# Layer 2 of a four-layer image network: two two-axis passes replaced by four one-axis passes on small array tiles, set between the next image's q, k and v

## The chip, the cores and the metric

The kernel runs on one core of one Trainium2 chip. The time is the device time of one execution in microseconds; the kernel before took 3720.93 us (median of three runs, 3720.22 to 3722.40). All data are float32, so every matmul on TensorE shows as two instruction records (two passes). The engines are called PE (TensorE), DVE (VectorE), ACT (ScalarE), POOL (GpSimd) and SP (SyncE, which issues most DMAs).

## The reference

Eight images of 512 channels and 32 x 32 pixels go through four layers:

```python
# layer 0
h = group_norm(x)                                  # 8 groups
q, k, v = split(qkv_w @ h + qkv_b)
h = softmax(q k^T / 8) v                           # 8 heads of 64
for _ in range(3):
    h = h + 0.1 * tanh(inl_w @ h + inl_b)          # the "inner loop"
x = x + proj_w @ h + proj_b
# layer 1
q, k, v = Wq @ x, Wk @ x, Wv @ x                   # q, k: 64 channels
x = x + v softmax(k-q scores)
# layer 2
out = x + bias
out = fir(fir(out, 2 * up_filter, up=2, axis=3), 2 * up_filter, up=2, axis=2)
out = leaky_relu(out, 0.2) * sqrt(2)
out = fir(fir(out, down_filter, down=2, axis=3), down_filter, down=2, axis=2)
# layer 3
rw = sigmoid(mean(out, pixels) @ router_w.T + router_b)     # 8 numbers per image
W = sum over e of rw[e] * experts[e]                         # mixed weights per image
... a bottleneck of three convolutions with W, three of batch normalization
```

Layer 2 treats each channel by itself: 32 x 32 pixels become 64 x 64, pass a leaky relu, and become 32 x 32 again. The filters have 12 taps. The same filter is used along both axes, so each pass can be done as one two-axis operator or as two one-axis operators.

## The kernel before

**Order of the work.** A loop over the images does layers 0, 1 and 2 of one image after another; layer 2's output z goes to DRAM ("spill"). Layer 3 follows for all images. Engines run concurrently, each through its own list of instructions. Where `tc.manual_schedule(engines=...)` stands, the listed engines keep the order in which the code is written; elsewhere a scheduler orders them.

**Products of 512 x 512 x 1024** (q, k, v, each inner step, proj, layer 1's values) use the seven products of Strassen's scheme in Winograd's form (`product`). They come in the order P1, C11, U2, U3, C22, C21, C12, each in two halves u = 0 and 1, and the generator yields after each of these 14 steps, so that callers can put other work between them. PE needs quarter sums of the operand (DVE) and copies of P1 (ACT). The accumulators are two banks of `ps_mm` (A) and the two double banks of `ps_sc` (X and Y); two more banks are in `ps_tp`. These eight banks are all of PSUM. Layer 1's weighted rows (`weighted_rows`) use the same scheme, written out.

**Layer 2 before.** The rows y (pixels x channels) are written to a padded copy in DRAM (`ypad`), and read back as overlapping blocks of 9 x 14 pixels with the pixels on the partitions (`Halo`). For each of 8 strips t of rows and 4 blocks c of columns one matmul with a 126 x 128 operator makes 8 x 16 fine pixels of 512 channels (`upsample`, L1139). ACT multiplies by 0.2 sqrt 2 and DVE takes the maximum (`leak`, L1122 and L1123). Then 256 matmuls per image, with the fine pixels as weights (128 x 64 tiles, two beside each other) and the down operator as moving data, add up into z with the channels on the partitions (`down_block`, L1157); an extra strip handles the last fine row. PE's order is written by hand: 3 strips up, rows down, 2 up, down, 3 up, down. The next image's statistics are made between layer 1's products, and q of the next image starts after layer 2.

**The experts.** Image b - 1's router and its mixed weights are made while q, k and v of image b run (`premix`): 9 pieces (the last of half the width), each of a 1 MB load on SP's queue, 16 scalings on ACT (L314) and additions on POOL (L319), with three pieces in flight. ACT and SP are in hand order there. The inner loop and proj of before have nothing beside them.

**Big buffers.** Tensors of 2 MB rotate through a pool of seven (`big_tile`); tensors of half a megabyte through six (`tmp`); weights through three.

Of the kernel before, what the change touches and what calls it, by code (L numbers as in the profile page):

```python
# [30 lines left out]
UR, UC = 8, 16  # L31
IR, IC = 9, 14
OR, OC = 9, 14
EDGE = 3
NT = 8
# [20 lines left out]
def tile_sequence(ctx: ExitStack, tc: tile.TileContext, a: dict, out: bass.AP, shifted: bool):  # L56
# [71 lines left out]
    up_op = const.tile([P, UR * UC], F32, name="up_op")  # L128
    up_left_op = const.tile([P, UR * UC], F32, name="up_left_op")
    dn_op = const.tile([P, OR * OC], F32, name="dn_op")  # L130
    up63_op = const.tile([P, P], F32, name="up63_op")
    nc.vector.memset(up63_op, 0.0)
    dn63_op = const.tile([P, 3 * W], F32, name="dn63_op")

    def layer2_constants():
# [5 lines left out]
        def scratch(name, n):  # L141
# [4 lines left out]
        counts = {  # L146
            "part": ([1, 1], 0, 1), "tap": ([1, NTAP], 0, 0),
            "first_in": ([IR, (P - 1) // IR], IR, 0), "first_up": ([UC, (P - 1) // UC], UC, 0),
            "first_in63": ([3, (P - 1) // 3], 3, 0),
            "ur": ([-1, UR], 17, 0), "uc": ([1, UC], 11, 0), "ucl": ([1, UC], 11 - 2 * EDGE, 0),  # L150
            "dr": ([2, OR], -6, 0), "dc": ([2, OC], 0, 0),
            "ur63": ([0, 1], 10, 0), "uc63": ([1, 2 * W], 5, 0),
            "dr63": ([2, 3], 1, 0), "dc63": ([2, W], 6, 0),
        }
        for name, (pattern, base, per_partition) in counts.items():
            t = counts[name] = scratch(name, pattern[1])
            nc.gpsimd.iota(
                t, [pattern], base=base, channel_multiplier=per_partition,
                allow_small_or_imprecise_dtypes=True,
            )  # L160

        taps_up, taps_dn = scratch("taps_up", NTAP), scratch("taps_dn", NTAP)
# [3 lines left out]

        def wide(t, n):
            return t.unsqueeze(1).to_broadcast([P, n, NTAP])

        def placed(name, idx, taps):  # L170
            n = idx.shape[1]
            t = scratch(f"placed_{name}", n)
            at = apart[:, 0 : n * NTAP].rearrange("p (n k) -> p n k", k=NTAP)
            nc.vector.tensor_tensor(
                at, idx.unsqueeze(2).to_broadcast([P, n, NTAP]), wide(tap, n), ALU.is_equal
            )
            nc.vector.tensor_tensor(at, at, wide(taps, n), ALU.mult)
            nc.vector.tensor_reduce(t, at, AX.X, ALU.add)
            return t

        tap, part = counts["tap"], counts["part"]

        def rows_of(name, width):

            row = scratch(f"row_{name}", 1)
            first = counts[f"first_{name}"]
            nc.vector.tensor_scalar(first, first, part, None, ALU.is_le)
            nc.vector.tensor_reduce(row, first, AX.X, ALU.add)
            col = scratch(f"col_{name}", 1)
            nc.vector.scalar_tensor_tensor(col, row, float(-width), part, ALU.mult, ALU.add)  # L190
            return row, col

        def tap_index(name, mul, by):

            t = counts[name]
            add = scratch(f"add_{name}", 1)
            nc.vector.tensor_scalar_mul(add, by, float(mul))
            nc.vector.tensor_scalar_add(t, t, add)
            return t

        def outer(op, rows, cols):
            nr, ncol = rows.shape[1], cols.shape[1]
            nc.vector.tensor_tensor(
                op.rearrange("p (r c) -> p r c", c=ncol),
                rows.unsqueeze(2).to_broadcast([P, nr, ncol]),
                cols.unsqueeze(1).to_broadcast([P, nr, ncol]),
                ALU.mult,
            )

        yield
        in_c, in_r = rows_of("in", IR)
        indices = {name: tap_index(name, -2, in_r) for name in ("ur",)}
        indices |= {name: tap_index(name, -2, in_c) for name in ("uc", "ucl")}  # L220
        yield
        up_rr, up_cc = rows_of("up", UC)
        indices |= {"dr": tap_index("dr", 1, up_rr), "dc": tap_index("dc", -1, up_cc)}
        yield
        in_c, in_r = rows_of("in63", 3)
        indices |= {
            "ur63": tap_index("ur63", -2, in_r), "uc63": tap_index("uc63", -2, in_c),
            "dr63": counts["dr63"], "dc63": tap_index("dc63", -1, part),
        }
        yield  # L230
        rows = {}
        for op, row, col, taps in (
            (up_op, "ur", "uc", taps_up), (up_left_op, "ur", "ucl", taps_up),
            (dn_op, "dr", "dc", taps_dn), (up63_op[:, 0 : 2 * W], "ur63", "uc63", taps_up),
            (dn63_op, "dr63", "dc63", taps_dn),
        ):
            if row not in rows:
                rows[row] = placed(row, indices[row], taps)
                yield
            cols = placed(col, indices[col], taps)  # L240
            outer(op, rows[row], cols)
            yield


    ypad = [
        spill.tile([(H + 5) * W, C], F32, name=f"ypad_{run}_{i}", tag=f"ypad_{i}") for i in range(2)
    ]


    rim0 = tmp("rim0")  # L250
    nc.gpsimd.memset(rim0, 0.0)
    def late_loads():
        nc.sync.dma_start(v_row, a["v_b"].partition_broadcast(P))
        nc.sync.dma_start(row_bias, a["bv"].partition_broadcast(P))
        nc.sync.dma_start(bias2, a["bias"].partition_broadcast(P))
        for t in ypad:
            nc.sync.dma_start(t[0 : 3 * W], rim0[0 : 3 * W])
            nc.sync.dma_start(t[(H + 3) * W :], rim0[0 : 2 * W])
# [17 lines left out]
    def route(b, parts):  # L276
# [4 lines left out]
        )  # L281
        nc.scalar.activation(rw[:, b, :], rw[:, b, :], AF.Sigmoid)

    def premix(b, halves=False):

        half, slots = NE // 2, 2 if halves else 3
# [4 lines left out]
        def load(i):  # L291
            at, n = pieces[i]
            slot = i % slots
            if slot < 2:
                views[i] = [read[:, slot, ts(h, half), 0:n] for h in range(2)]
                nc.sync.dma_start(read[:, slot, :, 0:n], a["experts"][:, :, at : at + n])
                return
            views[i] = [
                sums(f"experts_{b}_{i}_{h}").rearrange("p (e n) -> p e n", e=half)[:, :, 0:n]
                for h in range(2)  # L300
            ]
            for h in range(2):
                nc.sync.dma_start(views[i][h], a["experts"][:, ts(h, half), at : at + n])
# [68 lines left out]
    def channel_stats(b, x):  # L372

        stats = sums(f"stats_{b}")[:, 0 : CC * 2 * 6].rearrange(
            "p (c h s) -> p c h s", c=CC, h=2
        )
# [5 lines left out]
        return mv  # L382

    def norm_factors(b, mv):
# [8 lines left out]
        nc.vector.tensor_add(dev, dev, var_c)  # L393
        ps = bank(ps_tp, f"gn_var_{b}")
# [8 lines left out]
        return mul, add  # L403

    def group_norm(b, x, mul, add):
        h = big_tile(f"h_{b}", [P, CC, S])
        for cc in range(CC):
            nc.vector.tensor_scalar(
                h[:, cc, :], x[:, cc, :], mul[:, cc : cc + 1], add[:, cc : cc + 1],
                ALU.mult, ALU.add,  # L410
            )
        return h
# [267 lines left out]

    def layer0(b, x, norm, w):
        h = group_norm(b, x, *norm)
        if b == 0:
            first_sums(*held["q"], h[:, CC - 1, 0:1])
        t = quarter_sums(f"h_{b}", h)
        if b == 0:
            w["q"] = first_rest(*held["q"])
            for key in "kv":
                w[key] = weight_sums(key, *held[key], t[3][1][:, 0:1])
        fixed = tc.manual_schedule(engines={mybir.EngineType.Activation, mybir.EngineType.SP}) if b else nullcontext()  # L690
        with fixed:
            q = big_tile(f"q_{b}", [P, CC, S])
            parts = product(f"q_{b}", w["q"], h, t, channels(f"q_{b}", q, qkv_b[:, 0:CC]))
            for _ in range(2):
                next(parts)
            mixing = iter(())
            if b:
                mixing = premix(b - 1)
                next(mixing)
                route(b - 1, router_sums(b - 1))  # L700
            for _ in range(2):
                next(mixing, None)
            all_of(parts)
            if b == 0:
                nc.vector.tensor_add(row_bias, row_bias, bias2)
# [5 lines left out]
            for _ in range(2):  # L711
                next(parts)
# [178 lines left out]
    def layer1(b, x, w, midway):  # L891
# [112 lines left out]
        for t in range(3, NT):  # L1004
            halo.load(t)
# [517 lines left out]
```

## Time and profile before

| what | value |
|---|---|
| median of three runs | 3720.93 us (3720.22 to 3722.40) |
| the profiled execution: its own time | 3719.28 us |
| its span in the profile | 3717.5 us |
| granted TensorE clock, mean | 0.999 |
| busy: PE, DVE, ACT, POOL | 99%, 66%, 38%, 12% |
| from one image's q to the next image's | 436.25 us (890.93 to 1327.18) |
| DMA | 328.93 MB, 88 GB/s over the span |

The columns of a group of instructions are: line, engine, operation, output and inputs with their shapes, count, then busy time and the mean length of one in ns, then the idle time of that engine just before them with what ended it. In the chain of waits each row is a start, a length and what held the end of the program at that time. A row of the windows view is a stretch, its length, then for PE, weight loads, DVE, ACT and POOL the busy time and the count, then the granted TensorE clock, the DMA engines' busy share and the GB/s. Matmuls overlap their neighbours, so the mean length of one is more than the time that one adds.

### The profile page before, as it was taken

How to read it: one execution, taken by the hardware profiler on the slowest of the kernel's cores; microseconds unless marked ns; L12 is line 12 of the kernel's file. 1: busy time of each engine (PE TensorE's matmuls, PEld its weight loads, DVE VectorE, ACT ScalarE, POOL GpSimd, SP SyncE). 2: the span in 40 equal slices, each digit the busy share in tenths (PEclk: the TensorE clock that was granted, in tenths of full speed). 3: DMA queues.
4: the chain of work that ended last, by engine and by line, in shares of the span. 5: the costliest groups of instructions: out<-in, count | busy, mean ns of one | idle time of the engine just before them, and what ended most of it. 6: DMA issues, size and time to landing. Idle time of an engine off the chain costs nothing.

```text
span 3717.5 us, 51349 instructions
## 1 busy us (share of the span) xinstructions
PE 3687.2 (99%) x20742; PEld 1966.8 (53%) x20742; DVE 2440.0 (66%) x3412; ACT 1429.5 (38%) x2286; POOL 441.4 (12%) x586
## 2 busy tenths in 40 slices
PE   8999999999999999999999999999999999999998
PEld 4346753475435763467534764347543575347643
DVE  4887548665686657766487655866577664876454
ACT  1631255214552245322562136521454224631364
POOL 4000040001300040000400013000310004001031
PEclk9999999999999999999999999999999999999999
DMA  5002440125201350023501152013510235001763
GB/s 207 22 1 88 135 155 1 43 75 172 89 1 63 121 171 25 1 83 108 187 1 43 52 180 105 1 62 100 170 47 1 82 105 191 1 0 42 235 232 141
DMA packets 168583, 328.93 MB, mean 88 GB/s; under 512 B 12864, under 2 KB 112208, under 8 KB 162192
## 3 DMA queue, kind: packets, MB, share of 16 engines
q1 hardware_dynamic: 149952, 292.72, 23.3%
q0 software_dynamic: 4416, 19.99, 1.4%
q10 hardware_dynamic: 13968, 12.85, 1.0%
q8 instruction: 165, 2.70, 0.3%
q14 instruction: 82, 0.67, 0.1%
HBM read 256.70 MB, written 68.81 MB: 88 GB/s over the span
## 4 chain that ended last, share of the span: by engine, by line
PE 97%; DVE 2%; DMA 1%; ACT 0%; issue 0%; SPq 0%; ACTq 0%
PE scores L756 12%; PE av L797 12%; PE inl_X L527 6%; PE up L1139 5%; PE dn L1157 5%; PE v_X L527 5%; PE inl_Y L527 4%; PE av_X L1073 4%; PE inl_A L527 4%; PE v_Y L527 3%; PE av_A L1073 3%; PE v_A L527 3%; PE av_Y L1073 3%; PE proj_X L527 2%; PE q_X L527 2%; PE c L1339 2%
## 5 line engine op out<-in xcount | busy, mean ns | idle before, releaser
L775 ACT ACTIVATE e<-scores 128x1024 f32<-128x1024 f32 x504 | 516.1, 1024 | 441.7 <-PE scores L756 434.8
L756 PE MATMUL scores<-q,k 64*64 64x512 f32 x4096 | 531.9, 592 | 0.0
L797 PE MATMUL av<-e,v 64*64 64x512 f32 x4096 | 528.7, 589 | 0.0
L781 DVE TENSOR_TENSOR acc<-acc,e 128x1024 f32<-128x1024 f32 x320 | 389.2, 1216 | 36.7 <-ACT e L775 34.7
L319 POOL TENSOR_TENSOR experts<-experts 128x256 f32<-128x256 f32 (+2 forms) x297 | 237.8, 815 | 964.4 <-ACT experts L314 843.9
L756 PEld LDWEIGHTS scores<-q,k 64*64 64x64 f32 x4096 | 150.6, 133 | 295.3 <-issue 217.0
L797 PEld LDWEIGHTS av<-e,v 64*64 64x64 f32 x4096 | 156.6, 133 | 282.8 <-issue 277.2
L527 PE MATMUL inl_X<-T_hf,w_inl 128*128 128x512 f32 x576 | 261.8, 593 | 0.3 <-DVE inl_U L634 0.3
L314 ACT ACTIVATE experts<-experts,rw 128x256 f32<-128x256 f32 (+1 forms) x576 | 229.5, 483 | 80.1 <-DMA experts<-in_experts_dram 75.7
L1123 DVE SCALAR_TENSOR_TENSOR up<-up,leak 128x512 f32<-128x512 f32 x264 | 173.8, 687 | 128.7 <-ACT leak L1122 122.0
L959 POOL TENSOR_TENSOR seen<-seen,acc 128x512 f32<-128x512 f32 x16 | 20.2, 1264 | 1947.0 <-DVE acc L951 1946.4
L1122 ACT ACTIVATE leak<-up 128x512 f32<-128x512 f32 x264 | 149.8, 596 | 233.0 <-DVE up L1123 126.6
L818 DVE RECIPROCAL inv<-av 128x256 f32<-128x256 f32 x128 | 222.9, 1747 | 1.7 <-PE av L810 1.7
L1157 PEld LDWEIGHTS dn<-dn_op,up 128*64 128x64 f32 (+1 forms) x4096 | 187.9, 136 | 18.2 <-issue 18.2
L1157 PE MATMUL dn<-dn_op,up 128*64 128x99 f32 (+5 forms) x4096 | 194.1, 253 | 0.0
L623 ACT ACTIVATE inl_U<-inl_U,inl_b 128x512 f32<-128x512 f32 x96 | 66.7, 718 | 303.6 <-DVE inl_U L638 303.6
L527 PEld LDWEIGHTS inl_X<-T_hf,w_inl 128*128 128x128 f32 x576 | 108.6, 190 | 139.4 <-issue 114.5
L1139 PE MATMUL up<-halo,up_op 126*128 126x512 f32 (+1 forms) x384 | 179.7, 596 | 2.4 <-DVE up L1123 2.4
L527 PE MATMUL inl_A<-hf,w_inl 128*128 128x512 f32 x384 | 174.3, 596 | 0.0
L779 DVE TENSOR_TENSOR acc<-e,e 128x1024 f32<-128x1024 f32 x64 | 79.4, 1241 | 107.6 <-ACT e L775 77.3
L634 DVE TENSOR_TENSOR inl_U<-inl_X,inl_P 128x512 f32<-128x512 f32 x96 | 61.7, 684 | 105.1 <-PE inl_X L527 105.0
L527 PEld LDWEIGHTS inl_A<-hf,w_inl 128*128 128x128 f32 x384 | 71.6, 190 | 97.2 <-issue 86.1
(307 smaller groups left out, 5764.6 us busy)
## 6 DMA issues: line engine op xcount, KB each, us to landing
experts<-in_experts_dram SPq DMA_DIRECT2D x50, 1024.0 KB
halo<-ypad_u SPq DMA_DIRECT2D x128, 252.0 KB
halo<-ypad_u SPq DMA_DIRECT2D x128, 198.0 KB
w_v<-stored_u_v SPq DMA_DIRECT2D x14, 1792.0 KB
x<-in_x_dram SPq DMA_DIRECT2D x32, 512.0 KB
out_dram<-z SPq DMA_DIRECT2D x31, 512.0 KB
experts<-in_experts_dram SPq DMA_DIRECT2D x29, 512.0 KB
spill_u<-z SPq DMA_DIRECT2D x28, 512.0 KB
```

The costliest lines, as they stand in the source:

```text
L314: nc.scalar.activation(t[:, e, :], t[:, e, :], AF.Copy, scale=rw[:, b, which : which + 1])
L319: nc.gpsimd.tensor_add(dst, x, y)
L527: nc.tensor.matmul(dst, lhs, rhs, start=(opens and s == 0 and cc == 0), stop=(cc == 1 and s == rows), skip_group_check=True,)
L756: nc.tensor.matmul(ps[r][rows[c]], k[rows[r], oc, jc * P + c * HD : jc * P + c * HD + HD], q[rows[r], oc, ts(sh, HALF)], start=True, stop= ...
L775: nc.scalar.activation(e, pair, AF.Exp, scale=HD ** -0.5)
L781: nc.vector.tensor_add(accs[g], accs[g], e)
L797: nc.tensor.matmul(avs[g][r][rows[c]], v[rows[r], jc, ts(2 * oc + c, HD)], e[rows[r], ts(c, HALF)], start=(jc == 0), stop=(jc == SC - 1),)
L818: nc.vector.reciprocal(copies[g][:, at], totals[g][:, at])
L1073: nc.tensor.matmul(ps[:, ts(s, QR)], left[:, j, at : at + P], right[:, j, :], start=(what in ("P1", "U2", "W") and s == 0 and j == 0), sto ...
L1123: nc.vector.scalar_tensor_tensor(dst, ps, SQRT2, t, ALU.mult, ALU.max)
L1139: nc.tensor.matmul(ps[i], op[0 : IR * n, :], halo.tile(t)[0 : IR * n, c + i, :], start=True, stop=True,)
L1157: nc.tensor.matmul(rows[part, r0 - first : r1 + 1 - first, c0 : c1 + 1], up[t][0:k, c, ts(2 * cc + s, HD)], op[:, r0 - 4 * t + 3 : r1 + 4 ...
```

## The change

Layer 2 is done in four one-axis passes, by the class `Layer2`:

- `wide`: along the rows' pixels, 32 to 64. The operator is 32 x 64; eight matmuls of 32 x 64 array tiles (four row groups, two column groups) with 512 columns make one call, four calls make an image. The result goes to DRAM (`across`, two halves e of the channels) and comes back with the other axis on the partitions (`turn`).
- `up`: along the other axis, 32 to 64, eight units per image of eight 32 x 64 tiles each. ACT multiplies 128 x 1024 by 0.2, DVE takes the maximum (`tensor_max`), twice per unit.
- `down`: the same axis, 64 to 32, eight 64 x 32 tiles per unit, two units behind `up`. ACT copies one bank and DVE the other; the result goes to DRAM (`back`) and comes back turned (`turn_back`). `fine_passes` runs the units.
- `narrow`: along the first axis, 64 to 32, four calls of eight 64 x 32 tiles, copied by DVE; then `channels` transposes 128 x 128 blocks (32 per image) and ACT reads them out with the sum over pixels, which the router needs. `finish` runs both.

`between` sets these into the next image's work, with PE, DVE, ACT and SP in hand order: two wides inside `weighted_rows` (whose products come in a new order: P1, C11, U2, U3, C21, C22, C12), one before q, one after q's first step; `fine_passes` after q; k; `finish`; v, and the router after v's second step. For the last image `last_across` and `last_layer2` do the same with nothing in between.

The group norm of the next image is done in place on ACT instead of into a new tensor on DVE, and its statistics lie between the weighted rows' products. Because x is overwritten, it is loaded a second time for the residual of proj. The mixing of the experts of image b - 1 moves to the inner loop and proj of image b, one piece at every third product step, with two pieces in flight. The router's sigmoid is written ahead of it; in the built program ACT's list has it before the first exp of the attention, each with a load of its function table.

The core of the diff:

```diff
     def premix(b, halves=False):
-        half, slots = NE // 2, 2 if halves else 3
+        half, slots = NE // 2, 2
...
-        all_of(inner)
-        for it in (1, 2):
...
+        with tc.manual_schedule(engines=set(fixed)) if b else nullcontext():
+            mixing = iter(())
+            if b:
+                routed(b - 1)
+                mixing = premix(b - 1)
+                next(mixing)
+            slot = 0
+            def mix():
+                nonlocal slot
+                slot += 1
+                if slot % 3 == 2:
+                    next(mixing, None)
+            for _ in inner:
+                mix()
+            for it in (1, 2):
+                t = quarter_sums(f"hf_{b}_{it}", hf)
+                name = f"inl_{b}_{it}"
+                parts = product(name, w["inl"], hf, t, inner_step(name, hf))
+                for i, _ in enumerate(parts):
+                    mix()
...
+    def up(self, e, i):
+            n = 4 * e + i
+            pairs = []
+            for p in range(2):
+                if (2 * n + p) % 3 < 2:
+                    pair = ps_sc.tile([P, S], F32, tag="scores", ...)
+                    pairs.append(([pair[:, ts(r, HALF)] for r in range(2)], pair))
+                else:
+                    pairs.append(([bank(...) for r in range(2)], None))
+            for s in range(2):
+                for g in range(4):
+                    part = slice(W * g, W * g + W)
+                    first = 4 * i + 2 * s
+                    nc.tensor.matmul(
+                        pairs[g // 2][0][g % 2][HD * s : HD * s + HD, :], up_v[part, :],
+                        self.turned[e][part, first : first + 2, :], start=True, stop=True,
+                    )
+            fine = self.fine[n] = [tmp(f"fine_{self.b}_{n}_{p}", S) for p in range(2)]
+            for (banks, pair), t in zip(pairs, fine):
...
+                for dst, ps in parts:
+                    nc.scalar.mul(dst, ps, 0.2)
+                    nc.vector.tensor_max(dst, ps, dst)
...
+    def fine_passes(self):
+            order = [(e, i) for e in range(2) for i in range(4)]
+            lag = 2
+            for n in range(len(order) + lag):
+                if n < len(order):
+                    self.up(*order[n])
+                if n >= lag:
+                    e, i = order[n - lag]
+                    self.down(e, i)
+                    if i == 3:
+                        self.turn_back(e)
...
+    def between(b, eT, v, inv, y, x, w):
+        two = Layer2(b)
+        act, dve = nc.scalar.copy, nc.vector.tensor_copy
+        with tc.manual_schedule(engines=hand):
+            made, factors, stats = [], None, channel_stats(b + 1, x)
+            for what, u in weighted_rows(b, eT, v, inv, y):
+                if (what, u) in (("C11", 1), ("U2", 0), ("U2", 1), ("U3", 0)):
+                    mv = next(stats)
+                elif (what, u) == ("U3", 1):
+                    two.wide(0, 0, y, (ps_mm, ps_tp), (act, act))
+                    factors = norm_factors(b + 1, mv, made)
+                elif (what, u) == ("C21", 0):
+                    next(factors)
+                elif (what, u) == ("C22", 0):
+                    next(factors)
+                    two.wide(0, 1, y, (ps_mm, ps_tp), (act, act))
+                    two.turn(0)
+                elif (what, u) == ("C22", 1):
+                    group_norm(x, *made, nc.scalar)
+                    early_exp(b + 1)
+            two.wide(1, 1, y, (ps_mm, ps_tp), (act, dve))
+            t = sum_tiles(f"h_{b + 1}")
...
+            q, parts = queries(b + 1, x, t, w)
+            next(parts)
+            two.wide(1, 0, y, (ps_sc, ps_tp), (act, act))
+            two.turn(1)
+            all_of(parts)
+            w["inl"] = weight("inl", b + 1)
+            two.fine_passes()
+            k, parts = keys(b + 1, x, t, w)
+            all_of(parts)
+            w["proj"] = weight("proj", b + 1)
+            two.finish()
+            v, parts = values(b + 1, x, t, w)
+            next(parts)
+            sums_of = router_sums(b)
+            next(parts)
+            route(b, sums_of)
+            all_of(parts)
+            w["v1"] = weight("v1", b + 1)
+        return q, k, v
```

## The prediction

> **What bounds the kernel now.** I read the page first: its span, its busy line, the chain by engine and the costly groups.
>
> ```profile
> span 3717.5 us, 51349 instructions
> ...
> PE 3687.2 (99%) x20742; PEld 1966.8 (53%) x20742; DVE 2440.0 (66%) x3412; ACT 1429.5 (38%) x2286; POOL 441.4 (12%) x586
> ...
> PE 97%; DVE 2%; DMA 1%; ACT 0%; issue 0%; SPq 0%; ACTq 0%
> ...
> L775 ACT ACTIVATE e<-scores 128x1024 f32<-128x1024 f32 x504 | 516.1, 1024 | 441.7 <-PE scores L756 434.8
> ...
> L781 DVE TENSOR_TENSOR acc<-acc,e 128x1024 f32<-128x1024 f32 x320 | 389.2, 1216 | 36.7 <-ACT e L775 34.7
> ...
> L314 ACT ACTIVATE experts<-experts,rw 128x256 f32<-128x256 f32 (+1 forms) x576 | 229.5, 483 | 80.1 <-DMA experts<-in_experts_dram 75.7
> ...
> L1123 DVE SCALAR_TENSOR_TENSOR up<-up,leak 128x512 f32<-128x512 f32 x264 | 173.8, 687 | 128.7 <-ACT leak L1122 122.0
> ```
>
> TensorE is the bound everywhere: 99% busy, 97% of the chain. So only two things count: PE work that goes, and PE idle time that comes. Next, the chain of waits through layer 2 of image 3:
>
> ```profile
> 1271.92 3.47 PE av_X L1073 x16
> ...
> 1279.04 5.42 PE up L1139 x12
> 1284.46 8.46 PE dn L1157 x186
> 1292.92 7.07 PE up L1139 x16
> 1299.99 6.36 PE dn L1157 x128
> ...
> 1306.35 10.55 PE up L1139 x24
> ...
> 1327.18 7.20 PE q_A L527 x16
> ```
>
> The last av product ends at 1275.39 and q begins at 1327.18: 51.8 us, and 1.92 us of `up` ran earlier between the av products. So layer 2 holds PE for 53.7 us per image, nearly all of it work: 33 `up` matmuls of 0.86 us (28.4) and 24.2 of `dn`. The timeline of an attention stage shows what small tiles do:
>
> ```profile
> 1403.39 1.04 PE L756 MATMUL scores<-q,k 64*64 64x512 f32 x8
> ...
> 1404.25 1.04 PE L797 MATMUL av<-e,v 64*64 64x512 f32 x8
> ```
>
> Four 64x64 matmuls (two records each) start every 0.86 us, the time of one full-array matmul of 512 columns, and 1.04 us pass until the last ends. Last, two windows, q after layer 2 and an inner-loop step:
>
> ```profile
> 1327.00:1352.00 25.00, 25.00 (x65) 10.98 (x60) 11.21 (x19) 11.25 (x25) 10.16 (x13) 1.00 0.80 256
> 1545.00:1569.00 24.00, 24.00 (x57) 10.61 (x56) 16.12 (x27) 6.45 (x10) 0.00 (x0) 1.00 0.00 1
> ```
>
> PE (first pair after the span) is full in both; ACT (fourth) has slack, and DMA (the share before the GB/s) is 0.80 against 0.00.
>
> **The change part by part, per image.**
>
> *Removed:* the 53.7 us above. The halo reads and y rows, 9.5 MB, go too; they were hidden.
>
> *PE work added.* 4 wide calls, 8 up and 8 down groups, 4 narrow calls, each eight tiles of 32x64 or 64x32. A price for eight tiles is not in the trace. Low end: all eight together, 0.86, as four do; it can't be less, since 512 columns take two passes of 0.43 in every row. High end: four at a time, 1.73. I take 0.86: in the `dn` rows a record comes every 44 ns (8.46 us / 192), so issuing 16 in 0.86 us (54 ns) is no limit, and four tiles already run fully side by side. 24 groups are 20.6 us; 32 transposes at the xT row's 0.107 are 3.4. Sum 24.0, or 29.7 us less PE work than before.
>
> *Idle time added.* (a) The wides: 3.4 us of work; q's P1 can't have its banks before ACT and DVE have copied wide(1,1), two copies of 0.58 behind each other, so +1.3: 4.7.
>
> (b) Fine passes, between q and k with nothing else on PE. A unit needs two of the three PSUM pair buffers, so the second half of up(n+1) waits until DVE is through with pair 0 of up(n). The loop: semaphore to PE 0.055, the group to its last end 1.10 (1.04 above, plus four more starts), to ACT 0.07, `mul` of 128x1024 1.02 (L775's row), to DVE 0.03, `max` 1.25 (L781's 1.22; 1.26 to 1.29 where a 1024-wide operand came from PSUM): 3.5 us. Where pair 0 lies in two single banks (units 1, 4, 7) ACT and DVE overlap by halves, 3.15. DVE alone needs 2 x 1.25 and a copy of 0.65, 3.15; ACT 2.6. First max done 4.5 us after q, then 4 x 3.5 + 3 x 3.15 = 23.4, then the last max, down and its start 2.4: **30.3 us**, with 13.8 of PE work in it. So 16.5 of the 29.7 us saved come back here, as gaps of some 2 us.
>
> (c) Finish: 3.4 narrow, 3.4 transposes, 2.4 of waits for DVE's copies (0.65 each) and one ACT read: 9.2.
>
> (d) Experts mixing moves to the inner loop. Its cost in q, k, v was nil (PE full), so taking it out gains nothing. Its new slots: every third product step, 8 ACT scalings of 0.40 start to start, 3.3 us in front of whatever ACT does next. Most fall where ACT has 17 us free of 24. The one at slot 5 stands before the two copies of P1 that open inner step 1; DVE's quarter sums are due just then and PE's next product waits: 3.2 us. The one at slot 11, 0.65. Others, proj and their POOL adds (5.0 us a piece, POOL idle there) 0. If the expert load is late, ACT, which takes its queue in order, holds the tanh too; DMA is idle in that window and SP's eight extra issues have no one behind them until w_q, so 0. Bounds for (d): 0 (ACT catches up) to 8 (three chunks exposed).
>
> (e) The router's sigmoid now stands before the first exp of the attention: another table load on ACT, 1.28 us in its row, 1.0 on the path. Bounds 0 to 2.6.
>
> (f) Group norm goes from four DVE operations (0.80) to four on ACT (about 1.1), under av's products: 0. x is therefore read again, 2.1 MB and four SP issues, used 70 us later: 0. wide's writes, two turns and two returns are 16.8 MB instead of 9.5. q and its neighbours would move some 24 MB in 100 us, 240 GB/s, below the 256 that the window above shows. turn(1) lands about 22 us after q starts and q takes 26; turn_back(1) needs 12 us and k takes 24. Cost 0; with that cover gone, each microsecond late is paid once an image, up to 12 (0.5 MB written and 2.1 MB read at 256/0.80 = 320 GB/s are 8, and two landings 4, a guess).
>
> (g) The av products in a new order, C21 before C22 and C12, with the statistics of the next x (eight DVE operations of 0.67) between them: still 3.5 us of PE per product, and DVE has slack there, 0; were DVE late once, 1.3, one pair of its additions (0.69 each). Layer 2's operators of image 0 are fewer and lie under the inner loop as before, 0.
>
> Sum: 4.7 + 30.3 + 9.2 + 3.9 + 1.0 = 49.1 against 53.7, **-4.6 us** in each of seven images. The last image has no q and k to cover the turns: 3 for what is left of turn(0) after the wides, 12 for turn_back(1): 4.7 + 3 + 30.3 + 12 + 9.2 = 59, +5. Total -32 + 5 = -27 from the profiled execution's own 3719.28: 3692. The median, 3720.93, lies 1.65 above that execution, well inside the range.
>
> **A rule against the change.** The chain's very first q_A (14.76 us, after a nearly idle PE) took 10.19 us for sixteen records; the later one took 7.20. So this PE is slow after idling, and no later stage of before has a half idle PE. The Trainium skill, "TensorE: Matmul & The Clock Gate", Part 1, says that the clock halves after an idle window of about 3.4 us. By it gaps of 2 us cost nothing, and the sum stays. The same page's section on psum-queue depth-cycling says that frequent micro-idling between groups makes the clock oscillate. By that, (b) pays the first rival's price. No row of before decides between them.
>
> **Rivals.**
>
> *R1, slower: PE's clock drops in the fine passes.* For it: the slow first q_A. Against: gaps of 2 us, not 14. Price: the two passes of a group take 1.72 instead of 0.86, so the loop grows by 0.86 in 8 units, 7 us, and k starts cold, 3.0 (10.19 less 7.20): +10 an image, 80 in all, 3772. It decides from +3.4 an image (27 / 8), a third of that.
>
> *R2, slower: eight tiles go four at a time.* For it: nothing wider than four streams is shown, and all eight read their own 512 columns. Against: nothing in the spacing of `dn`. Price: 8 x 0.87 in the loop, 8 x 0.87 in wide and narrow, 14 an image: 3803. "TensorEngine Tiling (Array Packing)", Tiling Modes, of the Trainium skill, counts both shapes as eight independent tiles; by it R2 is out, and no row here shows it.
>
> *R3, about equal or a little slower: more chunks are exposed, or a turn is late.* For it: ACT, SP and DMA queues are all in order, and (d) and (f) are worked out with nothing late. 4 to 6 us an image more: 3720 to 3735, which includes the change not moving the time.
>
> *R4, much faster: the waits overlap better.* Fine passes at DVE's 3.15 a unit (28.5 in place of 30.3), the chunk of slot 5 hidden (3.2), half the waits of wide and finish (1.9): -7 an image more, 3645.
>
> **How the numbers follow.** Forecast as worked out 0.38 (3670 to 3710 by itself), R4 0.19, R3 0.16 (a quarter of it within 0.2%), R1 0.17, R2 0.10. A difference under 0.2% (7.4 us) can't be told from none here. Faster: 0.38 + 0.19 and a little of R1 with a clock that falls only now and then, 0.58. Same 0.04. Slower 0.38. Range: below 3625 only R4 with (e) hidden too; above 3785 R2 and a full R1 with late turns. So 3625 to 3785.
>
> **What the changed profile would show.** PE busy near 3687 - 8 x 29.7 = 3450, 93 to 94% of the span; `up` groups 3.1 to 3.5 us apart with idle ended by DVE's max; 8-tile groups of 16 records in 0.86 us; k's first products at the pace of q's; PE idle before inner step 1 ended by DVE or ACT; the granted clock at 1.00 in the fine passes (R1 wrong) or below; groups 1.7 us long (R2). I am wrong if idle shows up in q, k, v or the attention, where I have put none, or if `turned`/`back` reads end a wait.

## The result and the profile after

The changed kernel takes 4287.32 us (median of four runs, 4285.62 to 4290.46) against 3721.11 us. The ratio is 1.152, with a 95% interval of 1.150 to 1.154. The prediction was 3692 us in a range of 3625 to 3785, so it is wrong in sign, and even the dearest rival (3803) is nearly 500 us too cheap.

The span, the busy line and the chain by engine and line, from the page of the changed kernel:

```profile
span 4284.1 us, 48178 instructions
...
PE 3712.2 (87%) x19321; PEld 1789.4 (42%) x19321; DVE 2519.1 (59%) x3268; ACT 1535.6 (36%) x2399; POOL 528.3 (12%) x576
...
PE 64%; DMA 19%; DVE 9%; ACT 3%; SPq 3%; issue 1%; ACTq 0%; DVEq 0%
DMA across_u<-wide 12%; PE av L742 10%; PE scores L701 10%; DMA back_u<-sent 5%; PE inl_X L473 5%; PE v_X L473 4%; PE av_X L1014 4%; PE v_Y L473 3%; PE inl_A L473 3%; PE v_A L473 3%; PE inl_Y L473 2%; DVE T_hf L434 2%; PE c L1369 2%; SPq L1057 2%; PE dn L1103 2%; PE up L1080 2%
```

PE was 97% of the chain and is now 64%. The first name on the chain is no longer a matmul but a DMA, the write of the wide results to DRAM (`across`), and the write of the down results (`back`) is fourth: together some 700 us of waiting. Third comes DVE, with 9%.

Where in an image does it happen? In the timeline I took the first matmul of each stage, and from these starts the length of each stage. The table gives image 2 (images 1 to 7 are within 4 us of it in each stage). The columns e1, e8 and e9 are versions that are explained below; in e9 the first `up` stands inside q and the first narrows inside k, so that its rows from q to finish compare with the others only as a sum.

| stage, us | before | change | e1 | e8 | e9 |
|---|---|---|---|---|---|
| q | 24.5 | 44.6 | 27.2 | 25.4 | 21.9 |
| fine passes | - | 47.7 | 35.1 | 32.5 | 31.0 |
| k | 24.0 | 25.9 | 25.9 | 24.2 | 22.0 |
| finish | - | 21.4 | 9.1 | 9.1 | 11.8 |
| v | 24.3 | 26.2 | 26.1 | 24.5 | 24.5 |
| attention | 118.2 | 119.2 | 119.2 | 118.2 | 118.2 |
| inner steps, proj, layer 1's values and scores | 137.0 | 149.1 | 148.4 | 137.6 | 137.5 |
| transposes and first two weighted products | 19.2 | 19.3 | 19.3 | 19.3 | 19.3 |
| first av_X to the next q (before: with layer 2, 53.7) | 89.0 | 48.3 | 50.0 | 39.4 | 39.4 |
| sum | 436.3 | 501.7 | 460.3 | 430.1 | 425.7 |

The chain of the changed kernel between the weighted products and the second half of the fine passes, in order of time (start, length, what ended last):

```profile
1898.10 1.04 PE wide L1047 x16
...
1914.45 29.04 DMA across_u<-wide
...
1946.42 3.15 SPq L1057
1949.61 9.08 SPq L1057
1958.73 33.06 DMA across_u<-wide
1993.27 2.59 PE up L1080 x12
```

Two things stand here. The first row settles one rival at once: sixteen records of eight 32 x 64 tiles took 1.04 us, from the start of the first to the end of the last, as long as four 64 x 64 tiles. In the timeline the eight first passes start within 50 ns, and the eight second passes 0.43 us after the last of these. The other rows are waits of 29 and 33 us for writes of half a megabyte each, several behind one another. SP itself stands for 3 and 9 us on issuing such a write, with everything else in its queue behind it. The windows view says why (a stretch of 10 us during each write; the last two columns are the DMA engines' busy share and the GB/s):

```profile
1925.00:1935.00 10.00, 6.48 (x42) 2.28 (x43) 7.76 (x13) 2.42 (x5) 0.00 (x0) 0.99 0.13 53
1970.00:1980.00 10.00, 6.67 (x40) 1.92 (x38) 3.93 (x5) 1.02 (x1) 0.00 (x0) 0.96 0.13 54
```

The DMA engines are not busy: 0.13 is the share of two of sixteen. Nor do more writes at once help: four were issued between 1900.3 and 1920.2, and the rate stayed near 53 GB/s until the last had landed at 1943.6. The text before the prediction is wrong in one place: the generator `product` yields after each of its seven products, not after each of 14 halves; only `weighted_rows` yields 14 times.

### The profile page after: what moved, and what is told of

Read it like the earlier page. It is cut to its first block, busy times and chain, and to the rows that moved or that the text cites. A ratio compares the mean times of both kernels' runs of the same rounds, so it can differ in the third digit from the quotient of the medians.

```text
span 4284.1 us, 48178 instructions
## 1 busy us (share of the span) xinstructions
PE 3712.2 (87%) x19321; PEld 1789.4 (42%) x19321; DVE 2519.1 (59%) x3268; ACT 1535.6 (36%) x2399; POOL 528.3 (12%) x576
## 4 chain that ended last, share of the span: by engine, by line
PE 64%; DMA 19%; DVE 9%; ACT 3%; SPq 3%; issue 1%; ACTq 0%; DVEq 0%
DMA across_u<-wide 12%; PE av L742 10%; PE scores L701 10%; DMA back_u<-sent 5%; PE inl_X L473 5%; PE v_X L473 4%; PE av_X L1014 4%; PE v_Y L473 3%; PE inl_A L473 3%; PE v_A L473 3%; PE inl_Y L473 2%; DVE T_hf L434 2%; PE c L1369 2%; SPq L1057 2%; PE dn L1103 2%; PE up L1080 2%
## 5 line engine op out<-in xcount | busy, mean ns | idle before, releaser
L266 POOL TENSOR_TENSOR experts<-experts 128x256 f32<-128x256 f32 (+2 forms) x360 | 361.2, 1019 | 3044.7 <-ACT experts L261 3033.2
L720 ACT ACTIVATE e<-scores 128x1024 f32<-128x1024 f32 x504 | 516.1, 1024 | 384.6 <-PE scores L701 377.7
L1090 ACT ACTIVATE fine<-up 128x512 f32<-128x512 f32 (+1 forms) x168 | 127.6, 821 | 411.0 <-PE up L1080 259.4
L1091 DVE TENSOR_TENSOR fine<-up,fine 128x512 f32<-128x512 f32 (+1 forms) x168 | 156.2, 965 | 199.0 <-ACT fine L1090 194.9
L1080 PE MATMUL up<-turned,up_v 32*64 32x512 f32 x1024 | 141.4, 740 | 146.5 <-DVE fine L1091 124.4
L261 ACT ACTIVATE experts<-experts,rw 128x256 f32<-128x256 f32 (+1 forms) x576 | 230.6, 484 | 53.0 <-DMA experts<-in_experts_dram 47.7
L473 PE MATMUL inl_A<-hf,w_inl 128*128 128x512 f32 x384 | 185.6, 625 | 1.2 <-ACT inl_P L575 1.2
L1055 ACT COPY wide<-wide 128x512 f32<-128x512 f32 x110 | 58.0, 595 | 354.1 <-PE wide L1047 292.0
L473 PE MATMUL q_X<-T_h,w_q 128*128 128x512 f32 x192 | 100.8, 674 | 96.1 <-DVE q_U L505 96.1
L1136 PE MATMUL narrow<-back,dn_h 64*32 64x512 f32 x512 | 43.8, 771 | 113.5 <-DMA back<-back_u 113.5
L1155 ACT ACTIVATE z<-zT 128x1024 f32<-128x1024 f32 x32 | 32.6, 1022 | 298.2 <-PE zT L1151 256.1
L1080 PEld LDWEIGHTS up<-turned,up_v 32*64 32x64 f32 x1024 | 31.4, 149 | 252.8 <-DVE fine L1091 177.8
```

The source lines that it names most:

```text
L261: nc.scalar.activation(t[:, e, :], t[:, e, :], AF.Copy, scale=rw[:, b, which : which + 1])
L266: nc.gpsimd.tensor_add(dst, x, y)
L473: nc.tensor.matmul(dst, lhs, rhs, start=(opens and s == 0 and cc == 0), stop=(cc == 1 and s == rows), skip_group_check=True,)
L720: nc.scalar.activation(e, pair, AF.Exp, scale=HD ** -0.5)
L1080: nc.tensor.matmul(pairs[g // 2][0][g % 2][HD * s : HD * s + HD, :], up_v[part, :], self.turned[e][part, first : first + 2, :], start=True ...
L1090: nc.scalar.mul(dst, ps, 0.2)
```

## Experiments

Each version was timed once, and e8 (a second time) and e9 in five runs, which agree within 0.12%.

**e1: the writes split by their outermost count.** A wide result is written with 2 x 64 rows of 4 KB, a down result with 4 x 32. The experiment writes the same bytes in pieces that have 64 and 32 rows outermost:

```diff
-                nc.sync.dma_start(dst[:, :, first : first + S], t)
+                for h in range(2):
+                    nc.sync.dma_start(dst[h][:, first : first + S], t[ts(h, HD), :])
...
-            nc.sync.dma_start(dst[:, :, ts(i, S)], self.sent[e][:, ts(i, 4), :])
+            for g in range(4):
+                nc.sync.dma_start(dst[g][:, ts(i, S)], self.sent[e][ts(g, W), ts(i, 4), :])
```

> The changed kernel, with each write of a wide result issued as 2 DMAs of 64 rows and each write to back as 4 DMAs of 32 rows, the same bytes to the same places. Theory A (a DMA whose outermost count is 2 or 4 is spread over 2 or 4 of the 16 DMA engines; the trace shows a busy share of 0.13 and 53 GB/s during the wide writes): the shares rise, the waits on these writes go, 18 us in q, 17 in the fine passes, 12 in the finish and 4 of a slow clock in k and v per image, some 130 us in the last image: about 3800 us. Theory B (the writes are slow because of DRAM or of their 4 KB rows): no change, 4280. Theory C (PE, ACT and DVE themselves are slow in the fine passes): the waits on DMA go but the fine passes stay above 40 us: above 4000.

Measured: 3912.17 us, 375 less. The stages q, fine passes and finish fall by 17.4, 12.7 and 12.4 us per image, and the stretch from the last image's q to the end, which holds two layer 2s, by 117. The DMA issues of e1's page (KB each, then us from issue to landing):

```profile
across_u<-wide SPq DMA_DIRECT2D x128, 256.0 KB, 3.6
...
back_u<-sent SPq DMA_DIRECT2D x256, 128.0 KB, 2.3
```

Three times as many DMAs, the same bytes, and the median one lands in 3.6 and 2.3 us. Theory B, that DRAM or the 4 KB rows make the writes slow, is out, and so is theory C: the fine passes fall to 35.1 us. The kernel is still 5% slower than before, so this is not the only cause. Theory A had 3800: it was 112 us too low, because k and v did not recover, the fine passes stayed 4 us above my figure, and the last image's own layer 2, for which I had put 130, gave 74.

**e2: only the wide results' writes split.**

> As the one before, but only the writes of the wide results are split; the writes to back still have an outermost count of 4. Theory A: the finish still waits about 12 us per image for back, and the last image 40: 3900 to 3960 us. Theory B: 4280.

Measured: 4029.84 us, 70 us above the range, of the same sign; the finish still takes 21.7 us. This kernel shows the writes to `back` by themselves. The DMA view of 1430 to 1475 us, in 40 slices (busy share in tenths, then GB/s):

```profile
DMA  2110189999622222222222222222102999999999
GB/s 106 76 51 11 35 233 381 333 367 311 216 108 102 102 109 106 106 102 109 106 106 102 109 106 106 102 117 106 69 4 56 228 356 360 370 350 437 408 484 428
```

In the middle the writes with four rows outermost run alone: a share of 0.2 to 0.3, 102 to 109 GB/s. With two outermost it was 0.13 and 53. The reads on both sides, with 128 partitions outermost, run at 0.9 and 330 to 480. So for counts of 2 and 4 the rate goes with the outermost count, some 26 GB/s for each.

The Trainium skill states a rule for this, on which the prediction did not draw. "DMA: Bandwidth & Descriptors", in the section on why a DMA increments its semaphore by 16, says that a DMA is spread over the largest number of engines up to 16 that divides the slowest dimension of both sides, and its rules for kernel authors ask for a multiple of 16 outermost. The traces agree for 2 (0.13) and 4 (about 0.25).

**e3: e1 without most of POOL's additions.** Five of six additions per piece of the mixing are left out for images 0 to 6, so the mixed weights are incomplete:

```diff
             def added(dst, x, y):
-                nc.gpsimd.tensor_add(dst, x, y)
+                if halves or dst is mixed_to:
+                    nc.gpsimd.tensor_add(dst, x, y)
...
+            mixed_to = None
...
+            mixed_to = dst
             added(dst, lo[:, 0, :], lo[:, 1, :])
```

> The first kernel of this call, and in the mixing of images 0 to 6 five of six POOL additions per piece are left out (the mixed weights are incomplete); loads, ACT scalings and the writes stay. Theory A for the inner loop (POOL's additions slow DVE's quarter sums, which go from 0.68 to 1.21 us each beside them): the three inner steps fall from 83 to about 70 us per image, 85 us less than the first kernel in all. Theory B (ACT's scalings stand in front of the copies that open a step): no more than 20 us less in all, inner steps above 80.

Measured: 3855.64 us, 57 less than e1; the inner steps take 77.1 us in most images, proj 21.1. Both theories hold in part. From the inner steps to layer 1's scores the sum is 141.0 to 142.7 us (mean of seven images 141.5), against a mean of 150.3 in e1 and 137.0 before: the scalings, with the one addition that is left, cost 4.5, near the 3.9 that I had predicted, the other additions another 9. The timeline of the changed kernel shows their mechanism:

```profile
1734.13 3.28 ACT L261 ACTIVATE experts<-experts,rw 128x256 f32<-128x256 f32 x8
1735.17 1.28 DVE L434 TENSOR_TENSOR T_hf<-hf 128x512 f32<-128x512 f32 x2
1735.89 6.21 POOL L266 TENSOR_TENSOR experts<-experts 128x512 f32<-128x512 f32 x5 [13.16 <-ACT experts L261]
...
1738.05 1.21 DVE L434 TENSOR_TENSOR T_hf<-hf 128x512 f32<-128x512 f32 x1
...
1738.18 2.08 PE L473 MATMUL inl_X<-T_hf,w_inl 128*128 128x512 f32 x2 [3.48 <-DVE T_hf L434]
1739.18 1.21 DVE L434 TENSOR_TENSOR T_hf<-T_hf,hf 128x512 f32<-128x512 f32 x1
```

The two quarter sums that began before POOL did take 1.28 us together; of those beside it one takes 1.75 and the others 1.21 each, and POOL's five additions take 6.2 instead of 4.2 to 4.8. PE then waits 3.48 us for DVE. DVE's reads from PSUM are not slowed (`inl_U` takes 0.68 us in the changed kernel, beside POOL's additions as without them). That is what the Trainium skill, "SBUF — State Buffer", section "Who interferes with whom", states of a DVE operation with two inputs in SBUF beside GpSimd's reads.

**e4: e1 with a product on the other double bank after U2.**

```diff
-            ("U3", "X", s3, t3), ("C21", "X", a22, t4), ("C22", "Y", s1, t1),
+            ("W", "Y", s1, t1), ("C22", "X", s3, t3), ("C21", "X", a22, t4),
             ("C12", "Y", s4, b22),
```

The wide calls and the statistics inside the products move along with the new order.

> The first kernel of this call, with layer 1's weighted products in the order P1, C11, U2, W, C22, C21, C12, so that a product on the other double bank lies between U2 and the next product on U2's bank. Theory A (in the new order that next product waits until DVE, late behind sums and statistics, has read U2): the stretch from the first av_X to q falls by 8 to 10 us per image, 55 to 75 us less than the first kernel. Theory B (DVE is simply overloaded there by the statistics): less than 3 us per image.

Measured: 3892.18 us, 20 less; the stretch from av_X to q is only 1.6 us shorter. That is theory B's figure, but not its reason, which the timeline of this kernel contradicts:

```profile
1287.47 0.69 DVE L988 TENSOR_TENSOR av_U<-av_X,av_P 128x512 f32<-128x512 f32 x1
...
1288.21 5.41 PE L1014 MATMUL av_X<-T,S 128*128 128x256 f32 x16 [3.28 <-DVE av_U L988]
...
1306.31 0.69 DVE L993 TENSOR_TENSOR av_W<-av_X,av_W 128x512 f32<-128x512 f32 x1 [4.00 <-PE av_X L1014]
...
1307.05 3.72 PE L1014 MATMUL av_X<-v,eT 128*128 128x256 f32 x16 [0.67 <-DVE av_W L993]
```

PE waits before five of the ten half products on the double banks (3.28 us once, 0.67 to 0.78 otherwise), also where DVE had been idle for 4 us. The five are those that follow another half product on the same double bank directly; with a product on the other bank or a wide call in between there is no wait. The two halves of a double bank are one tile of the program, and the product on the one half waits until DVE has read the other. My theory had looked at whole products; the wait is between halves.

**e5: half of C22 between U2 and U3, in q, k and v.**

```diff
+            matmuls(which, (1,) if apart and what == "C22" else (0, 1))
+            if apart and what == "U2":
+                matmuls(4, (0,))
```

> The kernel with all writes split (e1), and in q, k and v of images 1 to 7 the first half of the product C22 (on the other double bank) is issued on PE between U2 and U3. Theory A (the hand order of PE put U3 right behind U2 on the same double bank, where before the scheduler had set half of C22 between; PE waits there for DVE's two additions): q, k and v each 1.4 to 1.9 us shorter, k at 24.1 and v at 24.3 us as in the kernel before, 30 to 40 us in all against e1. Theory B (k and v are slow from a PE clock that the fine passes and the finish leave low): no change in k and v, 25.9 and 26.1.

Measured: 3874.12 us, 38 less; q, k and v are 1.7 us shorter each, k 24.2 and v 24.5. Theory A holds, and a slow clock is out. In the kernel before, PE was not in hand order in these stages, and its trace has `k_Y` x4 between two groups of `k_X` x8: the scheduler had filled this wait.

**e6: the weighted products alternate by halves.**

```diff
+        for pair in (("P1",), ("C11",), ("U2", "W"), ("C22", "C12"), ("C21",)):
+            for u, what in [(u, what) for u in range(2) for what in pair]:
```

The order of the two channel halves e in layer 2 is exchanged, the statistics stand at other products, and the wide calls stand after W, C12 and C21.

> The kernel with all writes split (e1), and layer 1's weighted products alternate between the two double banks by halves (U2, W, U2, W, C22, C12, C22, C12, C21, C21), with the channel halves exchanged and the wide calls moved along. Theory A (a product may not write one half of a double bank before DVE has read the other; each pair in a row on one double bank costs 0.7 us, and 3.3 where DVE is late): the stretch from the first av_X to q falls from 48 to 51 to about 39 to 41 us, 60 to 75 us in all against e1. Theory B (DVE's work itself is the limit in that stretch): less than 3 us per image.

Measured: 3840.88 us, 71 less, and the stretch takes 40.9 us: theory A. DVE's operations are the same, so it is not their amount. Nor is it the wide calls that moved: in e1's trace (image 2) PE waits 7.1 us for DVE in this stretch and 0.74 for the copy of a wide, in e6's 0.67 for the copy of a wide and not for DVE. Where the clock does not fall behind the longest wait, e1's stretch takes 48.3 us, which is 7.4 more.

**e7: the nine pieces of the experts at other steps.**

```diff
-                if slot % 3 == 2:
+                if slot in (1, 2, 8, 9, 15, 16, 22, 23, 24):
```

> The kernel with all writes split (e1), with the same nine pieces of the experts mixed at other product steps: two in the middle of each inner step and three in proj, after the steps U2 and U3 (C22), where ACT has no copy or tanh due and DVE's quarter sums are not running. Theory A (the cost comes from where the pieces fall: scalings ahead of the copies of P1, POOL's additions beside the quarter sums): the three inner steps fall from 82.5 to 68 to 71 us per image, 80 to 100 us in all against e1. Theory B (ACT or POOL or the loads cannot keep this pace anywhere in the inner loop): above 77.

Measured: 3829.50 us, 83 less. The inner steps take 73.7 us against 66.5 before, and proj with layer 1's values less than before (boundaries move, since more work overlaps), in sum 137.5 against 137.0. The whole mixing costs 0.5 us where it no longer stands before the copies of P1 and all but one of its additions in an image miss the quarter sums, which are back at 0.684 us each. The one addition begins while DVE's quarter sums are under way, and there it is POOL that waits: 3.33 us instead of 1.28, and the four quarter sums beside it keep their 0.68. (In e3 one addition beside six quarter sums takes 4.08 us instead of 0.73 in the same way.) Here the quarter sums of the changed kernel:

```profile
L434 DVE TENSOR_TENSOR T_hf<-hf 128x512 f32<-128x512 f32 x128 | 106.4, 846 | 0.0
...
L434 DVE TENSOR_TENSOR T_hf<-T_hf,hf 128x512 f32<-128x512 f32 x64 | 62.7, 980 | 0.0
```

and of e7:

```profile
L434 DVE TENSOR_TENSOR T_hf<-hf 128x512 f32<-128x512 f32 x128 | 85.6, 684 | 0.0
...
L434 DVE TENSOR_TENSOR T_hf<-T_hf,hf 128x512 f32<-128x512 f32 x64 | 43.8, 684 | 0.0
```

**e8: all of these together**, with the sigmoid in v and a double bank of its own for the last but one down unit.

```diff
             route(b, sums_of)
+            routed(b)
+            early_exp(b + 1)
...
+            if n == 6:
+                pair = ps_sc.tile([P, S], F32, tag="scores", name=f"dn_{self.b}_{n}")
```

> All of these together (split writes, half of C22 between, alternating products, moved pieces), the router's sigmoid and the exp table's load in v instead of ahead of the attention (1 us), and the last but one down unit in a double bank of its own (1.5 us). If the effects add up: per image 461 less 10, 5, 13, 1 and 1.5, about 431; in all 3912 less 210: 3690 to 3720, about the kernel before.

Measured: 3690.15 us against 3718.56 for the kernel before, and a second time:

> The kernel with all changes (e8) again, timed against the kernel before in five rounds: 0.987 to 0.994 of the time before, as in its single execution (3690 against 3719 us).

3689.01 us, a ratio of 0.992 (0.990 to 0.993). The effects add up to what was expected (430.1 us per image for 431). Fine passes still took 32.5 us, and the windows of this kernel show part of the reason (the third column from the right is the granted clock):

```profile
1291.00:1297.20 6.20, 3.40 (x33) 0.77 (x32) 3.76 (x4) 1.94 (x2) 0.00 (x0) 1.00 0.78 291
1297.20:1301.30 4.10, 4.08 (x27) 0.94 (x32) 2.51 (x3) 2.00 (x3) 0.00 (x0) 0.52 0.03 11
1301.30:1305.00 3.70, 3.70 (x33) 0.83 (x34) 2.64 (x4) 2.53 (x4) 0.00 (x0) 0.61 0.00 0
1305.00:1312.00 7.00, 7.00 (x66) 1.50 (x66) 6.07 (x8) 5.27 (x8) 0.00 (x0) 1.00 0.59 149
```

PE works for 3.4 of the first 6.2 us, then runs at half its clock for about 7 us, and recovers while the passes go on. This happens in each of the seven images, and the longest gap between PE's records in these passes is 2.3 us (2.6 in one image).

**e9: the start and the end of the passes covered by q's and k's own products.**

```diff
+            for _ in range(5):
+                next(parts)
+            two.up(1, 0)
             all_of(parts)
...
+            two.fine_passes(begun=True, within=opened)
+            k, parts = k
+            for _ in range(5):
+                next(parts)
+            two.narrow(1, 0)
+            two.narrow(1, 1)
             all_of(parts)
```

`opened` issues k's first product ahead of the last down unit.

> The kernel with all changes (e8), and: the first up unit stands before q's last product C12 (on PSUM buffers that are free there), k's first product stands before the last down unit, and the first two narrow calls stand before k's last product. In e8 the fine passes take 32.5 us and the first units run at a granted clock of 0.52 to 0.61, after PE was idle for 2.8 of 6.2 us. Theory A (the passes start and end with PE waiting on ACT and DVE, and the idle start is what lowers the clock): the idle time is covered by q's and k's own products, the clock stays at 1.00, and an image takes 5 to 8 us less: 3635 to 3655 us. Theory B (any passes with PE half busy lower the clock; the dip only moves): 2 to 4 us per image, 3660 to 3676.

Measured: 3653.08 us (3650.25 to 3654.36), a ratio of 0.982 (0.980 to 0.983) to the kernel before, 36 less than e8, 4.4 per image in the table, a little below theory A's figure per image, and inside its range for the whole. Its fine passes in image 3:

```profile
1285.00:1293.00 8.00, 6.71 (x67) 1.25 (x66) 6.46 (x8) 5.46 (x9) 0.00 (x0) 1.00 0.52 211
1293.00:1301.00 8.00, 8.00 (x80) 1.76 (x80) 7.10 (x9) 5.73 (x9) 0.00 (x0) 1.00 0.66 171
1301.00:1309.00 8.00, 8.00 (x75) 2.25 (x70) 7.62 (x11) 5.60 (x9) 0.00 (x0) 1.00 0.58 156
```

The clock stays at 1.00 here and in images 1 and 6. In images 2, 4, 5 and 7 it falls to 0.5 for 3.4 us, some 10 us after the first `up`. Two windows of image 2:

```profile
857.00:861.80 4.80, 3.14 (x34) 0.65 (x32) 3.42 (x6) 2.00 (x3) 0.00 (x0) 1.00 0.69 239
861.80:865.20 3.40, 3.40 (x35) 0.55 (x25) 1.91 (x3) 2.34 (x3) 0.00 (x0) 0.50 0.48 205
```

With such a fall the passes take 30.7 to 31.2 us, without it 30.3. In the 3.4 us before these four falls PE's records cover 1.8 to 2.0 us, and 0.8 to 1.3 before the seven of e8. So the idle start did lower the clock, and covering it took away most of the slow time, but not all: theory B is not out, since passes with short gaps (at most 1.2 us in e9) still lower the clock in some images. The 4.4 us are waits that are now covered and a better clock together; no run separates them.

**e10: e9 with the writes joined again**, the diff of e1 taken back.

> The fastest version (e9) with the writes to DRAM joined again as in the change: outermost counts of 2 and 4. Theory A (the writes alone make the change slower than the kernel before, whatever the orders on PE and DVE): the 375 us that splitting gained in the changed kernel are lost again, all or nearly all of them: 3960 to 4060 us. Theory B (much of that was hidden waiting behind the other stalls, or is covered now because the turns are issued earlier): below 3850.

Measured: 4126.82 us, 474 more than e9, above the whole expected range. The writes alone make this design slower than the kernel before, and cost more where less else is waited for: here the finish waits 18 us instead of 12.

## Why the prediction was wrong, point by point

- **(f), the transfers: "Cost 0".** This is the step that failed. Of the 70 us by which a middle image missed (501.7 for 431.7), some 42 went when these writes were split (e1). I divided bytes by time (240 GB/s) and compared with what the trace had shown for other DMAs (256). That rate belongs to DMAs with 128 partitions outermost. These writes have 2 or 4 there and ran at 53 and 104 GB/s. The upper bound of 12 us went by the same kind of rate, so it was no bound. In the last image, where nothing covers the writes, the stretch from the first av_X to layer 3 grew by 90 us over before, for the 5 that I had put; in e1 by 16.
- **(g), the new order of the weighted products: 0, at most 1.3.** Wrong: 7.1 us of waits, and some 9 on average with the slow clock that follows the longest of them in four of seven images of e1 (e6). The step looked at DVE's slack, but not at what follows what on one double bank once PE is in hand order. The same reason cost 1.7 us in each of q, k and v (e5), which the prediction didn't list at all.
- **(d), the mixing: 3.9.** The scalings' part was nearly right (4.5 in e3); POOL's additions, put at 0, cost 9 by slowing DVE's quarter sums. The bound of 8 was too low. The rows of before hardly show it, since there most of POOL's additions lay beside reads from PSUM; but three 128 x 1024 sums of image 0's attention, whose two inputs are in SBUF, ran beside POOL and took 2.11 to 2.19 us instead of 1.22.
- **(b), the fine passes: 30.3.** 35.1 in e1. The loop is in the traces as worked out: once the passes run, a unit follows every 3.3 to 3.4 us in e1, for 3.15 to 3.5. Missing were the slow clock of the first units and the last three down units, which wait for one another's copies (e8's double bank for one of them gained at most 2.6 us).
- **(a), (c) and (e).** Finish 9.1 for 9.2, sigmoid 0.98 for 1.0. With the orders of (g) and e5 put right, the wides cost what was worked out: in e8 the stretch before q and q together take 5.0 us more than before without its layer 2, for 4.7. Taking the last image alone, e8 waits 14 and 6 us for its two turns, for 12 and 3.
- **R1, the clock.** In part right. Most of the slow clock of the change (its mean is 0.943, e1's 0.982) comes from the long waits for DMAs. But in e8 the clock fell in the fine passes without a gap above 2.6 us, so of the two places of "TensorE: Matmul & The Clock Gate" that were weighed, the one on an idle window of 3.4 us would not have foretold it, and the one on frequent micro-idling fits better. The price of R1 was too high: k starts at its usual pace in e8 (24.2 us), and in e9 a fall costs 0.4 to 0.9 us.
- **R2, eight tiles at a time four.** Out: 1.04 us for sixteen records.
- **R3, a late turn or more exposed pieces.** This is what happened; with (b), (g) and e5's waits it came to 65 us an image over before, where R3 had 4 to 6 more than the forecast.
- **PE's busy time** was expected at 3450 us; e9 still has 3588. In the fine passes of e9 the records fill a window of 8.00 us with 80 of them, five units' groups of sixteen: a group that waits in parts spreads over 1.4 to 2.0 us, with no idle time on record, instead of 0.86. That this is the whole difference is not shown.

The sum that was predicted, 3692, came out as e8, but that they meet is in part luck: in e8 the mixing costs 0.5 us and not 3.9, the sigmoid nothing and not 1.0, the fine passes 32.5 and not 30.3, and the last image's layer 2 is 12.5 us dearer than before and not 5.

## What to carry to other kernels

Look at the outermost count of both sides of every DMA that a change adds, before its bytes: with 2 or 4 there it ran at the share of two or four engines here, and an average of GB/s over other DMAs hides it. When an engine is put in hand order, ask what the scheduler had set between two steps on one buffer, half by half. Work that is moved under another stage must be priced against that stage's critical operations, by the memory that both read, and placed where they are not running.

## What the runs showed that I had not expected

- DMA writes of 512 KB ran at 53 GB/s with 2 rows outermost and 102 to 109 with 4, and SP stood up to 16.7 us on issuing one of them.
- POOL's additions and DVE's quarter sums, which read two SBUF tensors, slow one another: DVE's from 0.68 to 1.21 us, five of POOL's from 4.2 to 6.2. From PSUM, DVE kept its 0.68.
- Eight 32 x 64 tiles start within 50 ns and take no longer than four of 64 x 64.
- The granted clock fell to 0.5 in the fine passes of e8 after PE had been at work for 3.4 of 6.2 us, with no gap above 2.6 us, and came back within 7 us while the passes went on; in four of e9's images it fell with no gap above 1.2 us.
